# Attention blocks 2 to 4, tiles 20 to 29: two heads' sums of weights taken from pairs of tiles that GpSimd adds

## The chip, the cores and the metric

The kernel runs on one core of one Trainium2 chip. Times are device microseconds of that core. The chip runs five engines beside each other: TensorE (matrix products), VectorE, ScalarE, GpSimd and SyncE (which issues loads). They work on SBUF; TensorE writes its results to PSUM. The metric is the time of a whole execution, as the median over several runs.

## The reference, cut to what matters

A layer of graph attention with four heads over 4096 nodes, then a mixture of eight experts with the best two for each node. The change lies in the attention:

```python
h = jnp.einsum('nd,hdk->hnk', x, W)                     # 4 heads of 64
s_col = jnp.einsum('hnk,hk->hn', h, a1)
s_row = jnp.einsum('hnk,hk->hn', h, a2)
e = leaky_relu(s_row[:, :, None] + s_col[:, None, :], 0.2)
e = jnp.where(adj[None, :, :] > 0, e, NEG_INF)          # adj: 4096 x 4096 of 0 and 1
att = softmax(e, axis=-1)
h_prime = jnp.einsum('hij,hjk->hik', att, h)
```

So for each row i and head, two sums over the columns j are wanted: the weights times h (the numerator) and the weights alone (the denominator). Then follow an ELU, a residual, a layer norm, and for each node the choice of two experts, whose feed-forward results are added.

## The kernel before, in words

**Blocks and tiles.** The 4096 rows are worked in four blocks of 1024 (`NR = 4`; in the code block 1 is `a = 0`), each of two halves of 512. Over each block the kernel walks through 32 column tiles of 128 columns (`NT = 32`, index `j`). Columns lie on the partitions, rows along the free dimension.

**One tile.** SyncE loads 128 x 1024 of the transposed `adj` (`load_adj`, L1184). ScalarE turns it into a mask `am` in bfloat16, 0 or 2 (`mask_of`, L1606); there are three buffers. VectorE then makes the weights of one head at a time, for both halves together, in the order of heads 1, 0, 2, 3 (`weigh`, L1689): the larger of a row factor `er` and a column factor `eb`, cut by the mask. The exponentials have been split so that this needs no exponential in the loop; a factor that depends on the column alone is left out of the weights and is put on the other operand of the products, in `ha` (h of the column, times the factor) and `unit` (the factor alone, between columns of zeros). Weights `w` have ten buffers of 128 x 1024, that is two and a half tiles.

**The products.** For every tile, half and head TensorE multiplies `ha` by the weights (`rows_of_head`, L1198; two products of 32 columns each, added up in the four PSUM banks `acc`) and `unit` by the weights (`weights_of_head`, L1207; one product, added up in the bank `den`). [...] four products that use different columns can be under way together. An f32 product shows as two records, so a tile has 32 records of L1198 and 16 of L1207. `PLACE` says in which columns a head's sum of weights lies. The order of the products within a tile is written out by hand (`attend`) and chained by `queue`, so TensorE never changes it.

**What runs beside it.** While block n+1 is walked through, block n is finished a step at a time: `finish_blocks` is a generator, and after each tile the loop asks it for one more step (`next(pending)`). It divides (`shares_of`), applies ELU, residual and norms, and then routes (`route_rows`): transposes of the rows (L1253, evicted by L1256), the logits (L1264, evicted by L1269), their transposes (L1273), the choice of two experts on VectorE (L1280 to L1314), the place of each node in its expert's list (L1327 to L1345), and at last 16 indirect DMAs from GpSimd's queue that write the rows to the experts' lists in DRAM (L1385). In block 2, the first to be routed beside, a few steps more are made (two comparisons of 1024 elements, L1363). These steps take their PSUM from three shared banks with the tag `bank`.

**The order of work.** Apart from the chains written by hand, each engine's order is set when the program is built, by a planner that goes by the order in the code and its own estimates of time. On the chip each engine then works through its list in that order.

**Around it.** In block 4, after tile 3, a plan for the first experts is made and the rows of the first expert tile are loaded (L571); at tile 29 they are transposed (L607). After the attention comes the feed-forward phase, in which the last block is finished as well and its rows written to `xe`.

Of the kernel before, what the change touches and what calls it, by code (L numbers as in the profile page):

```python
# [18 lines left out]
P = 128  # L19
# [13 lines left out]
FINAL = (16, 15, 15, 15, 13, 13, 12, 9)  # L33
LIST = 36 * CH
PLACE = (2, 3, 0, 1)
ORDER = (1, 0, 2, 3)


# [6 lines left out]
def gat_then_moe(  # L45
# [173 lines left out]
    def forward(apart, stack):  # L219
# [16 lines left out]
        def first_large(name):  # L236
            return fin.tile([P, TB, D], F32, tag="first", name=name, bufs=2)
# [7 lines left out]
        def bank(shape, name):  # L245
            return ps.tile(shape, F32, tag="bank", name=name, bufs=3)
# [368 lines left out]
        with ExitStack() as layer:  # L615
# [588 lines left out]
            def weights_of_head(w, j, half, h):  # L1204
# [4 lines left out]
                    start=(j == 0 and half == 0), stop=(j == NT - 1 and half == HB - 1),  # L1209
                ))  # L1210

            def attend(w, j, halves, sums_first=None):


                def first_heads():
                    for half in halves:
                        for h in (1, 0):
                            rows_of_head(w, j, half, h)

                def other_heads():  # L1220
                    for half in halves:
                        for h in (1, 0):
                            weights_of_head(w, j, half, h)
                        rows_of_head(w, j, half, 2)
                    for half in halves:
                        rows_of_head(w, j, half, 3)
                        for h in (3, 2):
                            weights_of_head(w, j, half, h)

                parts = (first_heads, other_heads)  # L1230
                if sums_first is None:
                    sums_first = j in (0, NT - 1)
                for add in reversed(parts) if sums_first else parts:
                    add()

            def shares_of(pd):

                z = small.tile([P, TB, H, HB], F32, tag="z", name="z")
                for h in range(0, H, 2):
                    nc.vector.reciprocal(z[:, :, h : h + 2], pd[:, :, PLACE[h] : PLACE[h] + 2, :HB])  # L1240
                return z

            def route_rows(b, xe):
# [102 lines left out]
                if b == 0:  # L1346
# [33 lines left out]
                    yield  # L1380
                    nc.vector.tensor_tensor(others, others, least, OP.max)

                for t in range(n):
                    for k in range(2):
                        ins = nc.gpsimd.indirect_dma_start(  # L1385
                            lists, bass.IndirectOffsetOnAxis(ap=at[:, k, t : t + 1], axis=0),
                            xe[:, t, :], None,
                        ).ins
                        for i in listed:
                            tc.declare_no_dep(ins, i.name, reason="other places of the lists")  # L1390
                        listed.append(ins)

            def finish_blocks(a):
# [12 lines left out]
                for t in range(TB):  # L1406
                    order_of(nc.tensor.transpose(
                        pd[:, t].rearrange("p h q -> p (h q)"), ud[:, ts(t, P)], ident
                    ))
                z = shares_of(pd)  # L1410
                xe = rows_listed()
                n = HB * TB
                halves = [(half, slice(half * TB, (half + 1) * TB)) for half in range(HB)]
# [108 lines left out]
            def turn_sums(ud):  # L1522
                pd = bank([P, TB, H, Q], "pd")
                for t in range(TB):
                    queue(nc.tensor.transpose(
                        pd[:, t].rearrange("p h q -> p (h q)"), ud[:, ts(t, P)], ident
                    ))
                z = shares_of(pd)
                return z

            def last_block(b, u, z, given, xe):

# [146 lines left out]
            else:  # L1679

                with tc.tile_pool(name="sep", bufs=2) as work:

                    def weigh(er, am, j, halves):
# [10 lines left out]
                                w[half][h] = wh[:, half]  # L1694
                        return w

                    both = list(range(HB))
                    ers = [er0, er1]
                    er = er0
# [27 lines left out]
                        if j == 0:  # L1727
                            sums_turned(row)
                    for a in range(NR):
                        later = None  # L1730
                        for j in range(0 if a else TB, NT):
                            attend(
                                weigh(er, load_mask(a, j), j, both), j, both,
                                False if (a, j) == (NR - 1, NT - 1) else None,
                            )
                            if a == 0:
                                prepare_at(TB + j)
                            if pending:
                                next(pending, None)
                            if a == 1 and j == 1:  # L1740
                                turn_biases()
                            if a + 1 == NR and j == 3:
                                with tc.issue_after(marks["w"]):
                                    plan_early()
                                first_tile()
                            if a + 1 == NR and j == 29:
                                turn_first()
                                gelu_next(xT0[:, DC - 1, :1])
                            if j == 20 and a + 1 < NR:
                                later = ers[(a + 1) % 2]  # L1750
                                load_rows(later, (a + 1) * HB, HB, nc.scalar)
                        if a == 0:
                            mean_of_h()
                        er = later
                        if a + 1 < NR:
                            pending = finish_blocks(a)
                            next(pending)
# [351 lines left out]
```

## Time and profile before

| What | Value |
|---|---|
| Median of 3 runs | 1262.46 us (1262.27 to 1264.15) |
| The profiled execution's own time | 1260.56 us |
| Its span, first to last instruction | 1258.8 us |
| Granted TensorE clock | 0.999 |
| PE busy | 1241.7 us, 99% |
| DVE busy | 845.5 us, 67% |
| ACT busy | 448.3 us, 36% |
| POOL busy | 240.4 us, 19% |
| Attention, blocks 2 to 4, by TensorE's records | 256 to 782 us |

PE is TensorE, DVE VectorE, ACT ScalarE, POOL GpSimd, SP SyncE. In a line of the profile, L1198 is a line of the kernel, `out<-in` are tiles by the program's names, then come shapes and `xcount`. In a group's line the busy time, the mean of one in ns, and the engine's idle time before them with what ended it follow. In a line of the order of time the first number is the start in us, the second the length of the row, which may stand for several instructions one behind the other, and a bracket at the end holds the idle time before it and what ended that. Matmuls are pipelined and their ends are modelled, so that a busy PE isn't a PE at its peak.

### The profile page before, as it was taken

The page shows a single profiled execution, that of the slowest core. Times are in us where ns is not written, and L with a number is a line of the kernel's source. Part 1 is how long each engine was busy: PE and PEld are TensorE (multiplying, and loading weights), DVE is VectorE, ACT ScalarE, POOL GpSimd, SP SyncE. Part 2 cuts the span into 40 slices and gives each one's busy share as a digit, 9 for nine tenths or more (in the row PEclk, how much of TensorE's full clock was granted, in tenths as well). Part 3 has the DMA queues.
Part 4 walks back from the last instruction along what each step waited for, and adds up shares of the span by engine and source line. Part 5 has one row for each costly group of instructions (what it writes and reads, how often), then busy time and mean ns, then how long its engine had stood idle before and what let it go on. Part 6 is the DMA issues. An engine that isn't in the chain of part 4 may idle for free.

```text
span 1258.8 us, 22720 instructions
## 1 busy us (share of the span) xinstructions
PE 1241.7 (99%) x8872; PEld 650.4 (52%) x8872; DVE 845.5 (67%) x1566; ACT 448.3 (36%) x918; POOL 240.4 (19%) x217
## 2 busy tenths in 40 slices
PE   9999999999999999999999999999999999999997
PEld 5444444332233332333325324888888876666686
DVE  7998887879999999999999995855111111111120
ACT  4332322265522365322655221533332332222322
POOL 4000000001002601006110024125322222122222
PEclk9999999999999999999999999999999999999999
DMA  6334433536533646334375422868998895455662
GB/s 215 118 118 126 155 107 102 166 104 145 177 114 103 225 112 201 116 94 158 107 178 183 133 70 77 276 171 219 259 236 239 227 219 116 102 139 105 140 160 37
DMA packets 155541, 190.23 MB, mean 151 GB/s; under 512 B 72312, under 2 KB 125680, under 8 KB 155040
## 3 DMA queue, kind: packets, MB, share of 16 engines
q1 hardware_dynamic: 133392, 145.39, 39.7%
q0 software_dynamic: 20544, 36.74, 13.2%
q10 hardware_dynamic: 1488, 6.55, 1.4%
q8 instruction: 71, 1.16, 0.4%
q14 instruction: 46, 0.38, 0.1%
HBM read 155.77 MB, written 29.74 MB: 147 GB/s over the span
## 4 chain that ended last, share of the span: by engine, by line
PE 93%; DVE 3%; issue 1%; ACT 1%; DMA 1%; POOLq 0%; SPq 0%; DVEq 0%; ACTq 0%
PE acc L1198 33%; PE po L1906 18%; PE ph L1872 17%; PE den L1207 17%; PE pr L1053 2%; DVE w L1689 2%; PE ph L1101 2%; PE ptx L1253 0%; DMA early<-lists 0%; PE acc L894 0%; PE pt L780 0%; PE ptr L1491 0%; PE po L1945 0%; PE pl L1264 0%; PE po L875 0%
## 5 line engine op out<-in xcount | busy, mean ns | idle before, releaser
L1198 PE MATMUL acc<-w,ha 128*32 128x512 f32 x4096 | 672.1, 593 | 2.3 <-ACT u L1401 0.9
L1689 DVE SCALAR_TENSOR_TENSOR w<-er,eb,am 128x1024 f32<-128x1024 f32 x496 | 605.9, 1275 | 36.2 <-PE den L1207 30.3
L1207 PE MATMUL den<-w,unit 128*2 128x512 f32 x2048 | 469.2, 592 | 0.4 <-issue 0.3
L1198 PEld LDWEIGHTS acc<-w,ha 128*32 128x32 f32 x4096 | 186.7, 110 | 293.7 <-issue 254.3
L1606 ACT ACTIVATE am<-adj 128x1024 bf16<-128x1024 int32 x124 | 130.6, 1054 | 347.8 <-DVE w L1689 213.1
L1872 PE MATMUL ph<-xT,w 128*128 128x256 f32 (+5 forms) x864 | 230.2, 424 | 2.1 <-issue 1.9
L1906 PE MATMUL po<-w,hT 128*128 128x256 f32 (+1 forms) x1040 | 229.7, 379 | 0.0
L1876 ACT ACTIVATE hT<-ph,bias 128x256 f32<-128x256 f32 (+5 forms) x216 | 111.1, 517 | 290.2 <-issue 185.8
L1906 PEld LDWEIGHTS po<-w,hT 128*128 128x128 f32 (+1 forms) x1040 | 195.7, 189 | 31.2 <-issue 3.1
L1919 DVE SCALAR_TENSOR_TENSOR o<-po,share,b2s 128x256 f32<-128x256 f32 (+2 forms) x66 | 31.7, 482 | 250.2 <-PE po L1906 211.4
L1872 PEld LDWEIGHTS ph<-xT,w 128*128 128x128 f32 x864 | 163.4, 190 | 62.0 <-issue 40.3
L1207 PEld LDWEIGHTS den<-w,unit 128*2 128x2 f32 x2048 | 94.7, 85 | 148.5 <-issue 140.0
L1931 POOL DMA_INDIRECT out<-o,ids x66 | 102.0, 1546 | 321.9 <-DMA out<-o,ids 136.4
L1385 POOL DMA_INDIRECT lists<-xe,at x64 | 88.3, 1379 | 267.6 <-issue 184.7
L1856 DVE STREAM_TRANSPOSE xT<-xr 128x512 f32<-128x512 f32 (+5 forms) x21 | 17.8, 850 | 34.0 <-PE ph L1872 31.2
L1053 PE MATMUL pr<-wr,xT 128*128 128x256 f32 x128 | 30.4, 381 | 0.2 <-ACT er L1147 0.2
L1894 ACT ACTIVATE b2s<-b2b,share 128x256 f32<-128x256 f32 x68 | 30.1, 499 | 0.0
L1121 POOL DMA_DIRECT2D residual<-rb x6 | 4.7, 784 | 121.2 <-DVE rb L1068 121.2
L1441 POOL DMA_DIRECT2D xf<-in_x x6 | 8.1, 1351 | 102.2 <-ACT xf L1440 102.2
L1053 PEld LDWEIGHTS pr<-wr,xT 128*128 128x128 f32 x128 | 24.1, 190 | 5.4 <-issue 0.9
L1101 PE MATMUL ph<-wall,xT 128*128 128x264 f32 x96 | 24.6, 399 | 0.0
L207 ACT ACTIVATE m<-y,off 128x256 f32<-128x256 f32 x48 | 23.7, 495 | 1.1 <-DVE off L215 0.6
(394 smaller groups left out, 618.8 us busy)
## 6 DMA issues: line engine op xcount, KB each, us to landing
adj<-in_adj SPq DMA_DIRECT2D x126, 512.0 KB
w<-in_L_ffn_W SPq DMA_DIRECT2D x54, 1024.0 KB
er<-parts ACTq DMA_DIRECT2D x3, 2048.0 KB
lists<-zeros POOLq DMA_DIRECT2D x8, 520.0 KB
residual<-rb POOLq DMA_DIRECT2D x8, 512.0 KB
rb<-residual SPq DMA_DIRECT2D x8, 512.0 KB
out<-y POOLq DMA_DIRECT2D x8, 512.0 KB
xb<-in_x SPq DMA_DIRECT2D x7, 512.0 KB
```

Source lines behind the costliest of these rows:

```text
L1053: order_of(nc.tensor.matmul(pr[:, k, :], turned[b][:, c, ts(t0 + k, P)], wr[:, c, :], start=(c == 0), stop=(c == DC - 1),))
L1101: order_of(nc.tensor.matmul(phs[t - t0], xT[:, c, ts(t, P)], wall[:, c, :], start=(c == 0), stop=(c == DC - 1),))
L1198: queue(nc.tensor.matmul(acc[half][h // 2][here : here + Q, :], ha[:, j, h * K + g * Q : h * K + (g + 1) * Q], w[half][h], start=(j == 0), ...
L1207: queue(nc.tensor.matmul(den[here : here + HB, :], unit[:, j, h, 1 - half : 1 - half + HB], w[half][h], start=(j == 0 and half == 0), stop ...
L1385: ins = nc.gpsimd.indirect_dma_start(lists, bass.IndirectOffsetOnAxis(ap=at[:, k, t : t + 1], axis=0), xe[:, t, :], None,).ins
L1606: nc.scalar.activation(am, at, AF.Relu, scale=2.0)
L1689: marks["w"] = nc.vector.scalar_tensor_tensor(wh[:, these], er[:, these, h], eb[:, j, h : h + 1], mask[:, these], op0=OP.max, op1=OP.min,).ins
L1872: order_of(nc.tensor.matmul(ph, job["w1"][:, c, ts(f, P)], xT[:, c, :], start=(c == 0), stop=(c == DC - 1),))
L1876: job["gelu"] = nc.scalar.activation(hT[:, f, :], ph, AF.Gelu, bias=job["bias"][:, f : f + 1]).ins
L1906: order_of(nc.tensor.matmul(po[:size], hT[:, f, k * CH : k * CH + size], w2[:, f, :], start=(f == 0), stop=(f == FC - 1),))
L1919: given_out.append(nc.vector.scalar_tensor_tensor(o[:size], po[:size], share[:size, k : k + 1], b2s[k][:size], op0=OP.mult, op1=OP.add,).ins)
L1931: added.append(add().ins)
```

## The change

In blocks 2 to 4 every tile goes through new functions (`weigh_both`, `attend_both`), in block 1 none does. Three things are different.

First, the places of the sums of weights: each half has columns of its own now (`place_of`), and two heads share them. With that the order of the products in a tile is another: numerators of heads 1 and 0, then their sums of weights, then numerators of heads 2 and 3, then their sums. `shares_of` reads the new places.

Second, tiles 20 to 29 are taken as five pairs. In a pair the sums of weights of heads 1 and 0 are not made for each tile. Instead ScalarE multiplies the even tile's weights by the ratio of the two tiles' column factors (`ratio`), GpSimd adds the odd tile's weights (`added_pair`), and TensorE multiplies the odd tile's `unit` by that, once for each half and head, at the end of the odd tile. The added weights use two buffers of the tag `first`. In these tiles the mask is copied by ScalarE into one of two tiles of PSUM (`packed_mask`, two bfloat16 taken as one int32), which are two of the three shared banks, and VectorE reads it from there.

Third, the generator gives the word `"lists"` ahead of the list scatters, and the loop asks for the next step only from tile 30 on.

```diff
+PAIRED = (20, 30)
+ADDED = (1, 0)
...
+            def place_of(h, half):
+                return 2 * (h % 2) + half
+
+            def weights_by_half(w, j, half, h, start=False, stop=False):
+
+                here = place_of(h, half) * Q
+                queue(nc.tensor.matmul(
+                    den[here : here + HB, :], unit[:, j, h, 1 - h // 2 : 1 - h // 2 + HB],
+                    w[half][h], start=start, stop=stop,
+                ))
+
+            def attend_both(w, j, alone, summed=None, sums_first=False):
+
+                halves = range(HB)
+
+                def first_heads():
+                    for half in halves:
+                        for h in (1, 0):
+                            rows_of_head(w, j, half, h)
+
+                def other_heads():
+                    if alone:
+                        for h in (1, 0):
+                            for half in halves:
+                                weights_by_half(w, j, half, h, start=(j == 0))
+                    for half in halves:
+                        for h in (2, 3):
+                            rows_of_head(w, j, half, h)
+                    for h in (2, 3):
+                        for half in halves:
+                            weights_by_half(
+                                w, j, half, h, start=(j == 0 and not alone), stop=(j == NT - 1)
+                            )
+                    if summed:
+                        for h in ADDED:
+                            for half in halves:
+                                weights_by_half(summed, j, half, h)
...
+                if not ordered[0]:
+                    yield "lists"
                 for t in range(n):
                     for k in range(2):
                         ins = nc.gpsimd.indirect_dma_start(
...
+                    def packed_mask(am, j):
+
+                        pm = masks[j % 2]
+                        nc.scalar.copy(pm.bitcast(I32), am.bitcast(I32))
+                        return pm.bitcast(BF16)
+
+                    def weigh_both(er, a, j):
+
+                        am = load_mask(a, j)
+                        mask = packed_mask(am, j) if paired(j) else am
+                        w = [[None] * H for half in range(HB)]
+                        for h in ORDER:
+                            wh = work.tile([P, HB, B], F32, tag="w", name="w", bufs=10)
...
+                            made[j % 2][h] = wh
...
+                    def added_pair(j):
+
+                        w = [[None] * H for half in range(HB)]
+                        for h in ADDED:
+                            s = first_large("s").rearrange("p t d -> p (t d)")
+                            s = s.rearrange("p (s r) -> p s r", s=HB)
+                            nc.scalar.activation(
+                                s, made[0][h], AF.Copy, scale=ratio[:, j // 2, h : h + 1]
+                            )
+                            nc.gpsimd.tensor_tensor(s, s, made[1][h], OP.add)
+                            for half in range(HB):
+                                w[half][h] = s[:, half]
+                        return w
...
+                        if a == 1:
+                            pairs = unit[:, :, :2, 1].rearrange("p (n k) h -> p n k h", k=2)
+                            nc.vector.tensor_scalar(ratio, pairs[:, :, 1], TINY, None, op0=OP.max)
+                            nc.vector.reciprocal(ratio, ratio)
+                            nc.vector.tensor_tensor(ratio, ratio, pairs[:, :, 0], OP.mult)
+                            nc.vector.tensor_scalar(ratio, ratio, 1.0 / EPS, None, op0=OP.min)
...
+                            if a == 0:
+                                attend(weigh(er, load_mask(a, j), j, both), j, both)
+                            else:
+                                if j == PAIRED[0]:
+                                    masks = [bank([P, B], "pm") for k in range(2)]
+                                w = weigh_both(er, a, j)
+                                attend_both(
+                                    w, j, not paired(j),
+                                    added_pair(j) if paired(j) and j % 2 else None,
+                                    j == 0 or j == NT - 1 and a + 1 < NR,
+                                )
...
-                            if pending:
-                                next(pending, None)
+                            if pending and (step != "lists" or j >= PAIRED[1]):
+                                step = next(pending, None)
```

More of the change, by code (lines that the diff above doesn't have):

```diff
@@ L1210, in weights_of_head @@
                 ))
+            def place_of(h, half):
[29 more added lines that the diff above has]
+                                weights_by_half(summed, j, half, h)
+                parts = (first_heads, other_heads)
+                for add in reversed(parts) if sums_first else parts:
+                    add()
             def attend(w, j, halves, sums_first=None):
@@ L1234, in attend, with shares_of @@
                     add()
-            def shares_of(pd):
+            def shares_of(pd, by_half):
                 z = small.tile([P, TB, H, HB], F32, tag="z", name="z")
+                if by_half:
+                    for k in range(0, H, 2):
+                        nc.vector.reciprocal(
+                            z[:, :, k : k + 2].rearrange("p t h s -> p t (h s)"), pd[:, :, :, k // 2]
+                        )
+                    return z
                 for h in range(0, H, 2):
@@ L1409, in finish_blocks @@
                     ))
-                z = shares_of(pd)
+                z = shares_of(pd, apart and a > 0)
                 xe = rows_listed()
@@ L1527, in turn_sums @@
                     ))
-                z = shares_of(pd)
-                return z
+                return shares_of(pd, apart)
             def last_block(b, u, z, given, xe):
@@ L1695, in weigh, with paired @@
                         return w
+                    def paired(j):
+                        return PAIRED[0] <= j < PAIRED[1]
+                    def packed_mask(am, j):
[8 more added lines that the diff above has]
+                            wh = work.tile([P, HB, B], F32, tag="w", name="w", bufs=10)
+                            marks["w"] = nc.vector.scalar_tensor_tensor(
+                                wh, er[:, :, h], eb[:, j, h : h + 1],
+                                mask.rearrange("p (s r) -> p s r", s=HB), op0=OP.max, op1=OP.min,
+                            ).ins
+                            made[j % 2][h] = wh
+                            for half in range(HB):
+                                w[half][h] = wh[:, half]
+                        return w
[8 more added lines that the diff above has]
+                            nc.gpsimd.tensor_tensor(s, s, made[1][h], OP.add)
+                            for half in range(HB):
+                                w[half][h] = s[:, half]
+                        return w
+                    made = [[None] * H for k in range(2)]
+                    ratio = gat.tile([P, NT // 2, 2], F32)
                     both = list(range(HB))
@@ L1729, in forward @@
                     for a in range(NR):
[L1730 to L1735 removed]
+                        later, step = None, None
+                        if a == 1:
[4 more added lines that the diff above has]
+                            nc.vector.tensor_scalar(ratio, ratio, 1.0 / EPS, None, op0=OP.min)
+                        for j in range(0 if a else TB, NT):
+                            if a == 0:
[8 more added lines that the diff above has]
+                                    j == 0 or j == NT - 1 and a + 1 < NR,
+                                )
                             if a == 0:
                                 prepare_at(TB + j)
[L1738 to L1739 removed]
+                            if pending and (step != "lists" or j >= PAIRED[1]):
+                                step = next(pending, None)
                             if a == 1 and j == 1:
```

## The prediction

> **What bounds the kernel now.** I read the groups first, then the order of time on TensorE, VectorE, ScalarE and GpSimd through blocks 2 to 4 (256 to 782 us), last the chain. The groups name the two engines that matter: the products of the attention, and the weighting on VectorE that feeds them.
>
> ```profile
> L1198 PE MATMUL acc<-w,ha 128*32 128x512 f32 x4096 | 672.1, 593 | 2.3 <-ACT u L1401 0.9
> L1689 DVE SCALAR_TENSOR_TENSOR w<-er,eb,am 128x1024 f32<-128x1024 f32 x496 | 605.9, 1275 | 36.2 <-PE den L1207 30.3
> L1207 PE MATMUL den<-w,unit 128*2 128x512 f32 x2048 | 469.2, 592 | 0.4 <-issue 0.3
> ```
>
> A mean of 593 ns for a product is no price: four of them run side by side. The price is the distance from tile to tile, in TensorE's order of time where nothing else lies between:
>
> ```profile
> 571.92 1.90 PE L1198 MATMUL acc<-w,ha 128*32 128x512 f32 x16
> ...
> 577.07 1.90 PE L1198 MATMUL acc<-w,ha 128*32 128x512 f32 x16
> ...
> 582.22 1.90 PE L1198 MATMUL acc<-w,ha 128*32 128x512 f32 x16
> ```
>
> A tile takes 5.15 us for 48 records (each f32 product is two), four at a time: 12 slots of 0.429 us. VectorE's order of time gives its price per weighting and what else it does:
>
> ```profile
> 509.29 33.56 DVE L1689 SCALAR_TENSOR_TENSOR w<-er,eb,am 128x1024 f32<-128x1024 f32 x28
> 543.70 3.68 DVE L1689 SCALAR_TENSOR_TENSOR w<-er,eb,am 128x1024 f32<-128x1024 f32 x3 [0.84 <-PE den L1207]
> ...
> 554.77 0.21 DVE L1291 TENSOR_TENSOR oh<-lg,mm 128x64 f32<-128x64 f32 x1
> 554.90 0.15 DVE L1306 TENSOR_TENSOR d<-mm 128x8 f32<-128x8 f32 x1
> 555.02 0.23 DVE L1294 TENSOR_TENSOR oh<-oh,order 128x64 f32<-128x64 f32 x1
> ```
>
> 28 weightings in 33.56 us are 1.20 us each (the 1275 ns overlap), so 4.79 us a tile, plus small routing operations. So the engines are nearly level: TensorE sets the time, VectorE is only 0.36 us a tile faster, and loses that where routing or finishing falls to it. What keeps TensorE fed is a **head start**. I measure it as TensorE's first product of a tile minus the end of the tile's fourth weighting, counting four weightings and 48 records to a tile. In block 3 it is 3.85 us at tile 0, -2.08 at tile 9 (finishing work on VectorE), 4.37 at tile 20, 4.18 at tile 30. Block 2 has 4.58 at tile 20 and 3.12 at tile 30. Block 4 has 3.81 at tile 0, then -3.16 at tile 5 and -4.00 at tile 9, and there TensorE does wait for VectorE:
>
> ```profile
> 655.22 0.62 PE L1198 MATMUL acc<-w,ha 128*32 128x512 f32 x2 [0.40 <-DVE w L1689]
> ```
>
> VectorE's only slack is its waits for a free weight buffer (ten of them), as the 0.84 us above: at the head of block 3 they are 0.25, 1.67 and 1.44 us, at the head of block 4 0.25 and 1.68.
>
> [...] four products per 0.429 us slot. [...] The trace has no GpSimd arithmetic here, but its scatters fit: their issues last 2.08 us or 0.97, and the difference of 1.1 is about one weighting (two SBUF inputs).
>
> ```profile
> 578.35 2.08 POOL L1385 DMA_INDIRECT lists<-xe,at  x1 [0.30 <-issue]
> 580.73 0.97 POOL L1385 DMA_INDIRECT lists<-xe,at  x1 [0.30 <-issue]
> ```
>
> [...] start to start, the three-operand operation on 256 elements takes 395 ns from PSUM (L1063) and 397 from SBUF (L1564). [...]
>
> **The change part by part.** *Removed.* In a pair the sums of heads 1 and 0 go from 8 products to 4: 2 slots, 0.857 us. 15 pairs give 12.9 us, 4.29 a block. All of it is on the path while the head start lasts.
>
> *Order of products, tiles of blocks 2 to 4.* Still 12 slots, four columns filled in each: nothing. But heads 2 and 3 are now both wanted from slot 7, 2.57 us after the tile's start (head 3, made last, was wanted from slot 9, 3.43 us), and in paired tiles from slot 5, 1.71 us. So TensorE waits once the head start falls below about -2.6, or -1.7 in a pair.
>
> *Weighting with its mask in PSUM.* 120 of them; by the trace 0 more each. [...]
>
> *GpSimd's adds*, [...] the last is due at slot 11 of the odd tile. With head 1 of that tile weighted 1.7 us before the tile starts, [...] and the sum is wanted 4.29 us in. Hidden; it shows above about 3 us an add. Queued behind them on GpSimd are only the scatters.
>
> *Collisions.* The weightings no longer have two SBUF inputs, but routing has: the rows at 554.77 to 555.02 are such, and they fall into tiles 22 to 24, where the adds run. [...] I count two adds met in blocks 3 and 4 each (2.2 us) and four in block 2, whose tile 27 also has the two 1024-element comparisons L1363 (4.4 us). Ends: 0 to twice that.
>
> *ScalarE.* Per tile one copy of the mask into PSUM (0.58 us, the row of 512 elements at L1256), per pair two scalings of 1.06 us as L1606: 3.3 us more per pair of some 10 us, on an engine that is busy 10 to 13 us of the 55 in that stretch. The scalings wait for `s`, so for the pair before to end; masks queue behind them, and VectorE behind those. At a head start of 8 us for the first weighting this costs at most about 1.5 us a block, and it costs nothing once the start has shrunk; 0 to 1.5.
>
> *Scatters to tile 30.* The 16 issues take 25 to 33 us on GpSimd (572 to 601 in block 3) and begin some 13 us later, behind the adds; they end by tile 3 of the next block. Who wants them: the load of the first expert's rows on SyncE's queue at 632 us, and in the last block the rewriting of `xe` at 812, each more than 15 us after the new end; GpSimd's next own work comes at 627. Nothing. Reciprocals, ratios (four tiny operations once): nothing.
>
> **The sum**, as a ledger of the head start. *Block 2's pairs:* 3.12 - 4.29 - 4.4 = -5.6; floor -1.7, so TensorE waits 3.9. *Head of block 3:* from -1.7, +0.73 to tile 0 as before, is 4.8 below the old; the buffer waits vanish and give 3.4 back; tile 9 is at -2.08 - 1.4 = -3.5; floor -2.6: waits 0.9. *Block 3's pairs:* 4.37 - 0.5, -0.2 to tile 30 as before, +1.1 of vanished buffer waits, -4.29 - 2.2, is -1.7: no wait. *Head of block 4:* 4.9 below the old, 1.9 given back; tiles 5 to 9 have no room: waits 3.0. *Block 4's pairs:* 4.2 + 0.4 - 4.29 - 2.2 = -1.9: 0.2. Waits together 8.0; what is left of 12.9 is 4.9 us. Not every collision will be met; [...] and I take 5.5. The profiled execution took 1260.56 us (span 1258.8 and 1.8 around it), so 1255.1; the median of the runs is 1.9 above it, and the same gain gives **1257.0**.
>
> **The rivals.**
> *All of it stays:* collisions and ScalarE cost nothing, the adds are hidden. Then only the head of block 4 gives back, 1 to 3 us: 10 to 12, about 1251. For it: buffer waits of 3.4 and 1.9 us. Against: the routing rows lie where the adds run.
>
> *No change:* [...] about 1263. Against: 395 beside 397 ns.
>
> *Slower: masks wait for a bank.* Three banks are shared; two are now masks for ten tiles. VectorE starts tile 20 at 530.82, long before TensorE. But the transposes and logits of tiles 18 and 19 hold banks till later, until these rows end:
>
> ```profile
> 536.73 1.05 ACT L1256 COPY xT<-ptx 128x512 f32<-128x512 f32 x2
> ...
> 541.51 0.41 ACT L1269 COPY lT<-pl 128x128 f32<-128x128 f32 x2
> ```
>
> If banks are given in the order of the program, tile 20's mask waits until about 537.8 and tile 21's until 541.9: VectorE is 7 us late and the head start is gone before the first pair. In the ledger each block then waits 6 us more at its pairs (7 less the buffer wait of about 1 that vanishes): 18 in all against 5.5 gained, 12 slower, about 1275; half the delay, 3.5 us, gives about 1264. It decides from about 3 us. Against: the banks are free before tile 17, and masks prepared ahead could take them then; the routing would queue for the one left.
>
> *The sum isn't shortened* (other slots run empty): then nothing is gained and the waits stay; counted with the slower case.
>
> **How the numbers follow.** 0.2%, or 2.5 us, is about what a measurement of this kernel can tell from no change. Forecast (gain of 2.5 to 8) 0.44; all stays (over 8) 0.18; no change 0.14; slower 0.24, among it adds of over 3 us. So faster 0.62, same 0.14, slower 0.24. The range goes from 1250.5 (12 us gained, the whole removal less 0.9) to 1267.0, which leaves out the worse part of the banks' case.
>
> **What would show it.** Den records: 60 products, 120 records, fewer. Weightings in tiles 20 to 29 still 1.20 us apart. [...] The routing rows in tiles 22 to 24 with gaps or lengths of 1 to 2 us. Even paired tiles 4.29 us apart. Head start near -1.7 at tile 30 and TensorE waiting for w at tiles 5 to 9 of block 4. Wrong if the head start falls before tile 20, if adds take over 3 us, or if weightings from PSUM stand further apart.

## The result: 5.5% slower

The changed kernel takes 1331.56 us, the kernel before 1262.37 us beside it: a ratio of 1.0552 (95% interval 1.0531 to 1.0574). The prediction was 1257.0 us, range 1250.5 to 1267.0. The profiled execution took 1331.96 us (span 1330.2). Where the 71.4 us between the two spans lie, from the first product of tiles 0, 20, 27 and 30 in TensorE's order of time, summed over blocks 2 to 4, in us:

| | tiles 0-19 | 20-26 | 27-29 | 30-31 | attention ends at | span behind it |
|---|---|---|---|---|---|---|
| before | 330.8 | 111.6 | 49.0 | 34.4 | 781.9 | 476.9 |
| after | 334.4 | 130.3 | 96.1 | 33.0 | 849.6 | 480.6 |

Two thirds come in three tiles a block, 27 to 29, a quarter in tiles 20 to 26. The groups of the profile after (line engine op out<-in xcount | busy us, mean ns | idle before us and its releasers):

```profile
L1764 DVE SCALAR_TENSOR_TENSOR w<-er,eb,am 128x1024 f32<-128x1024 f32 x264 | 329.5, 1311 | 29.7 <-POOL s L1782 21.8 <-PE den L1220 7.2 <-PE den L1209 0.6
L1764 DVE SCALAR_TENSOR_TENSOR w<-er,eb,pm 128x1024 f32<-128x1024 f32 x120 | 147.1, 1274 | 15.8 <-ACT pm L1754 15.8
L1782 POOL TENSOR_TENSOR s<-s,w 128x1024 f32<-128x1024 f32 x30 | 70.6, 2372 | 217.3 <-DVE w L1764 180.7 <-DVE first L1346 21.5 <-DVE oh L1341 14.9
L1220 PE MATMUL den<-s,unit 128*2 128x512 f32 x120 | 31.2, 678 | 36.8 <-POOL s L1782 36.8
```

Products (L1200) and single sums wait little more than before; the new products, the sums of `s`, do: 36.8 us for GpSimd's adds (L1782). An add takes 2372 ns, so its length isn't the reason. Its place is. GpSimd's order of time in block 3:

```profile
603.06 1.04 POOL L1437 DMA_INDIRECT lists<-xe,at  x1 [4.41 <-DVE at L1395]
...
609.54 0.97 POOL L1437 DMA_INDIRECT lists<-xe,at  x1 [0.30 <-issue]
610.54 4.68 POOL L1782 TENSOR_TENSOR s<-s,w 128x1024 f32<-128x1024 f32 x2
615.39 1.00 POOL L1437 DMA_INDIRECT lists<-xe,at  x1 [0.16 <-issue]
...
619.24 7.04 POOL L1437 DMA_INDIRECT lists<-xe,at  x1 [0.31 <-issue]
...
632.97 0.97 POOL L1437 DMA_INDIRECT lists<-xe,at  x1 [0.30 <-issue]
633.95 4.65 POOL L1782 TENSOR_TENSOR s<-s,w 128x1024 f32<-128x1024 f32 x2
```

In block 3 six scatters stand in front of the adds of tiles 26 and 27, ten in front of those of tiles 28 and 29, and one of the ten lasts 7.04 us. The hold to tile 30 sits in the order of the program; the order in which GpSimd gets its work is the planner's. The first scatter goes out as soon as its indices `at` are there, and the adds come behind. (That the planner expected the adds later is likely, but not shown.) TensorE, in order, stops at the sum (11.48 us in its order of time, at the end of tile 29):

```profile
636.36 1.87 PE L1220 MATMUL den<-s,unit 128*2 128x512 f32 x4 [11.48 <-POOL s L1782]
```

and with it VectorE, whose weight buffers are not given back (its own order of time):

```profile
636.34 4.55 DVE L1764 SCALAR_TENSOR_TENSOR w<-er,eb,am 128x1024 f32<-128x1024 f32 x2 [10.91 <-POOL s L1782]
```

TensorE's waits for `s`, 36.8 us, all lie in tiles 27 to 29. A part of the rest of the loss there is the clock: from 421.9, 630.1 and 828.1 us, within the waits, the granted clock is 0.50 for 10.24 us each. In the kernel before it is 1.00 all through the attention. In the second of these stretches groups of products start 0.81 us apart, as the first two at 636.36 and 637.17 do, and a record lasts 1.01 to 1.06 us; at 1.00 it is 0.43 and 0.59. TensorE is busy for 12.9 us of the three stretches; by these distances about half of that, 6.5 us, is an estimate of what the lower clock costs.

Tiles 20 to 26 are lost on VectorE, in its order of time in block 3:

```profile
535.40 19.22 DVE L1764 SCALAR_TENSOR_TENSOR w<-er,eb,am 128x1024 f32<-128x1024 f32 x16
558.76 4.86 DVE L1764 SCALAR_TENSOR_TENSOR w<-er,eb,pm 128x1024 f32<-128x1024 f32 x4 [4.14 <-ACT pm L1754]
568.30 0.23 DVE L1330 TENSOR_TENSOR lg<-pg,bgb 128x64 f32<-128x64 f32 x1 [4.67 <-PE pg L1323]
569.07 9.62 DVE L1764 SCALAR_TENSOR_TENSOR w<-er,eb,pm 128x1024 f32<-128x1024 f32 x8 [0.55 <-ACT pm L1754]
...
581.25 1.39 DVE L1344 TENSOR_TENSOR oh<-oh,order 128x64 f32<-128x64 f32 x1
...
592.67 1.78 DVE L1361 TENSOR_SCALAR p<-th 128x8 f32<-128x8 f32 x1 [0.62 <-ACT th L1359]
```

Tile 20 waits 4.14 us for its mask. In ScalarE's order of time the copy of the mask follows directly on the last eviction of a transpose, and the next ones come behind those of the logits:

```profile
557.04 1.07 ACT L1306 COPY xT<-ptx 128x512 f32<-128x512 f32 x2 [0.31 <-PE ptx L1303]
558.14 0.59 ACT L1754 COPY pm<-am 128x512 int32<-128x512 int32 x1
...
563.68 0.27 ACT L1319 COPY lT<-pl 128x128 f32<-128x128 f32 x1 [0.17 <-PE pl L1314]
...
566.88 0.58 ACT L1754 COPY pm<-am 128x512 int32<-128x512 int32 x1
...
568.45 0.58 ACT L1754 COPY pm<-am 128x512 int32<-128x512 int32 x1
```

In the code the masks ask for their banks behind the transposes, so the bank is the likely reason; the trace can't tell it from the copy's place in ScalarE's own queue. Then a routing operation, `lg`, stands ahead of tile 21's weightings and waits 4.67 us for a product on TensorE. The weightings wait 0.55 us more, for a copy that ends at 569.03, so in this kernel the mask ends last here too. Together 9.4 us: the head start of block 3, 4.37 us at tile 20 before, is -0.2, and -3.5 at tile 21. Once a mask is there, eight weightings take 9.62 us, 1.20 each, as much as in the kernel before (28 in 33.56 us): here a mask in PSUM costs no more than one in SBUF. The last two rows of VectorE are operations that meet an add; in the kernel before they take 0.23 and 0.17 us.

### The profile page after: what moved, and what is told of

The parts are those of the page before. It is cut to its first block, busy times and chain, and to the rows that moved or that the text cites. A ratio compares the mean times of both kernels' runs of the same rounds, so it can differ in the third digit from the quotient of the medians.

```text
span 1330.2 us, 22649 instructions
## 1 busy us (share of the span) xinstructions
PE 1262.9 (95%) x8752; PEld 667.0 (50%) x8752; DVE 860.4 (65%) x1570; ACT 498.0 (37%) x978; POOL 300.0 (23%) x247
## 4 chain that ended last, share of the span: by engine, by line
PE 83%; POOL 5%; DVE 4%; issue 4%; ACT 2%; DMA 1%; POOLq 0%; SPq 0%; DVEq 0%; ACTq 0%
PE acc L1200 28%; PE po L2011 17%; PE ph L1977 16%; PE den L1220 9%; PE den L1209 4%; DVE w L1764 3%; POOL lists L1437 3%; PE pr L1055 2%; PE ph L1103 2%; POOL s L1782 2%; ACT s L1779 1%; PE ptx L1303 1%; DMA early<-lists 0%; PE acc L896 0%; PE pt L782 0%
## 5 line engine op out<-in xcount | busy, mean ns | idle before, releaser
L1200 PE MATMUL acc<-w,ha 128*32 128x512 f32 x4096 | 579.2, 600 | 8.8 <-DVE w L1764 7.2
L1764 DVE SCALAR_TENSOR_TENSOR w<-er,eb,am 128x1024 f32<-128x1024 f32 x264 | 329.5, 1311 | 29.7 <-POOL s L1782 21.8
L1200 PEld LDWEIGHTS acc<-w,ha 128*32 128x32 f32 x4096 | 169.9, 110 | 299.5 <-issue 214.7
L1220 PE MATMUL den<-w,unit 128*2 128x512 f32 x1296 | 201.1, 592 | 0.0
L1764 DVE SCALAR_TENSOR_TENSOR w<-er,eb,pm 128x1024 f32<-128x1024 f32 x120 | 147.1, 1274 | 15.8 <-ACT pm L1754 15.8
L1740 DVE SCALAR_TENSOR_TENSOR w<-er,eb,am 128x1024 f32<-128x1024 f32 x112 | 138.3, 1276 | 13.3 <-PE den L1209 13.3
L1782 POOL TENSOR_TENSOR s<-s,w 128x1024 f32<-128x1024 f32 x30 | 70.6, 2372 | 217.3 <-DVE w L1764 180.7
L1209 PE MATMUL den<-w,unit 128*2 128x512 f32 x512 | 117.6, 592 | 0.1
L1220 PEld LDWEIGHTS den<-w,unit 128*2 128x2 f32 x1296 | 45.4, 85 | 94.1 <-issue 79.6
L1437 POOL DMA_INDIRECT lists<-xe,at x64 | 76.4, 1193 | 31.5 <-issue 17.4
L1220 PE MATMUL den<-s,unit 128*2 128x512 f32 x120 | 31.2, 678 | 36.8 <-POOL s L1782 36.8
L1779 ACT ACTIVATE s<-w,ratio 128x1024 f32<-128x1024 f32 x30 | 33.1, 1144 | 42.1 <-PE den L1220 42.1
L1209 PEld LDWEIGHTS den<-w,unit 128*2 128x2 f32 x512 | 23.5, 85 | 38.8 <-issue 37.7
```

Of the source, the lines that this page charges most:

```text
L1200: queue(nc.tensor.matmul(acc[half][h // 2][here : here + Q, :], ha[:, j, h * K + g * Q : h * K + (g + 1) * Q], w[half][h], start=(j == 0), ...
L1209: queue(nc.tensor.matmul(den[here : here + HB, :], unit[:, j, h, 1 - half : 1 - half + HB], w[half][h], start=(j == 0 and half == 0), stop ...
L1220: queue(nc.tensor.matmul(den[here : here + HB, :], unit[:, j, h, 1 - h // 2 : 1 - h // 2 + HB], w[half][h], start=start, stop=stop,))
L1437: ins = nc.gpsimd.indirect_dma_start(lists, bass.IndirectOffsetOnAxis(ap=at[:, k, t : t + 1], axis=0), xe[:, t, :], None,).ins
L1740: marks["w"] = nc.vector.scalar_tensor_tensor(wh[:, these], er[:, these, h], eb[:, j, h : h + 1], mask[:, these], op0=OP.max, op1=OP.min,).ins
L1764: marks["w"] = nc.vector.scalar_tensor_tensor(wh, er[:, :, h], eb[:, j, h : h + 1], mask.rearrange("p (s r) -> p s r", s=HB), op0=OP.max, ...
```

## The experiments

In the expectations, theory A is that scatters ahead of the adds cost the time, theory C that the masks wait for a bank; the third candidate is that adds and VectorE keep each other out at SBUF. Sums in us over blocks 2 to 4 as above; ratios to the kernel before that ran beside each (medians of 1254 to 1263 us):

| | ratio (95%) | 20-26 | 27-29 | behind |
|---|---|---|---|---|
| e1, scatters behind adds | 1.0292 (1.0254-1.0331) | 130.6 | 48.4 | 488.8 |
| e2, order only | 1.0034 (1.0010-1.0059) | 111.6 | 47.5 | 478.4 |
| e3, masks only | 1.0372 (1.0329-1.0416) | 120.6 | 82.3 | 477.0 |
| e4, e1 from tile 22 | 1.0136 (1.0103-1.0168) | 116.2 | 48.4 | 486.7 |
| e5, e1 with masks in SBUF | 1.0515 (1.0479-1.0552) | 140.7 | 68.8 | 482.9 |
| e6, no hold | 1.0564 (1.0547-1.0581) | 130.3 | 94.9 | 478.1 |
| e7, e3 with fills | 1.0186 (1.0153-1.0220) | 120.7 | 48.7 | 486.7 |
| e8, e4 with fills | 1.0237 (1.0205-1.0268) | 116.2 | 48.4 | 501.4 |
| e9, before with fills | 1.0028 (1.0016-1.0040) | 111.6 | 47.5 | 481.9 |
| e10, blocks 2, 3 from tile 24 | 1.0105 (1.0087-1.0123) | 119.9 | 46.6 | 475.1 |
| e11, tiles 10 to 15 | 1.0050 (1.0034-1.0066) | 111.6 | 47.5 | 476.6 |
| e12, tiles 8 to 17 | 1.0084 (1.0059-1.0108) | 113.8 | 47.5 | 476.7 |
| e13, before, five fills | 0.9966 (0.9955-0.9977) | 111.6 | 47.4 | 478.1 |
| e14, masks only, 10 to 15 | 1.0020 (1.0008-1.0032) | 111.6 | 47.5 | 479.7 |

**e1: the scatters behind the last add.**

```diff
-                            nc.gpsimd.tensor_tensor(s, s, made[1][h], OP.add)
+                            marks["add"] = nc.gpsimd.tensor_tensor(s, s, made[1][h], OP.add).ins
...
-                        ins = nc.gpsimd.indirect_dma_start(
+                        with tc.issue_after(marks["add"]) if "add" in marks and not ordered[0] else ExitStack():
+                            ins = nc.gpsimd.indirect_dma_start(
```

> The changed kernel with one ordering edge more: in each block the 16 list scatters stand behind the last add of tile 29 on GpSimd's queue. Theory A (GpSimd's queue: scatters planned ahead of the adds of tiles 27 and 29 hold TensorE there, some 49 us over three blocks): 1280 to 1292 us, TensorE's waits for s below 3 us a block, the scatters start only after the tenth add. Rival B (the chain of scaling, add and sum is too long by itself, whatever stands in the queue): above 1310 us, tiles 27 and 29 still over 8 us long.

Tiles 27 to 29 go from 96.1 us to 48.4; TensorE's wait for `s` is gone, and the lower clock in these tiles with it: theory A is shown, at 48 us. About 8 of them come back behind the attention (488.8 us for 480.6), where the scatters of block 4 now run, and so the time, 1293.55 us, is just above the forecast.

**e2: the new order alone** (`paired` is always false, no mask banks, the hold kept).

> The changed kernel with no pairs, no adds and no masks in PSUM; the new places and the new order of the products stay, and the hold of the scatters. Theory A and theory C (the masks in PSUM start VectorE's tile 20 late for want of a bank): both say the order costs nothing, 1259 to 1265 us. Rival D (heads 2 and 3 being wanted earlier in a tile costs TensorE waits in blocks 2 to 4): 1266 us or more, with tiles over 5.4 us at tiles 5 to 17.

At most 0.6%: places, order and reciprocals are not the cause. The hold is in this kernel too, and still its scatters of block 3 begin at 573.24 us, against 572.02 before. So the hold doesn't delay them.

**e3: masks in PSUM for tiles 20 to 29, no pairs, no adds.**

```diff
-                        return PAIRED[0] <= j < PAIRED[1]
+                        return False
...
-                        mask = packed_mask(am, j) if paired(j) else am
+                        mask = packed_mask(am, j) if PAIRED[0] <= j < PAIRED[1] else am
```

> The changed kernel with the masks of tiles 20 to 29 copied to PSUM, but no pair and no add: every tile has its own sums. Theory C: the weighting of tile 20 or 21 still begins late, VectorE idles 8 to 10 us a block there, and with nothing saved on TensorE the time is 1272 to 1284 us. Rival: it is the scaling on ScalarE that delays the masks, so without it the masks come in time: 1260 to 1266 us and no idle time of VectorE at tile 20.

Tiles 20 to 26 lose 9.0 us in three blocks, and in block 3 VectorE idles 10.9 us there, with no scaling in the program: the delay of theory C, at a lower cost than expected. It has two parts. Tile 20 waits 5.41 us for its mask; then `lg` waits 5.53 us for TensorE, until 560.63, while the next two masks are done by 558.44, so here `lg` ends last. The time as a whole is above both forecasts. The surprise is 33 us in tiles 27 to 29, with no add in the program. There the scatters follow one another at 1.28 us, where in the kernel before about half of them stand some 2.4 us apart, and TensorE has holes that no semaphore explains (releaser "issue"), all while scatters are issued. TensorE's order of time in block 3:

```profile
605.26 0.63 PE L1200 MATMUL acc<-w,ha 128*32 128x512 f32 x2 [1.08 <-issue]
607.36 1.31 PE L1200 MATMUL acc<-w,ha 128*32 128x512 f32 x3 [1.47 <-issue]
609.50 1.03 PE L1200 MATMUL acc<-w,ha 128*32 128x512 f32 x2 [0.82 <-issue]
```

e2 has such holes too, smaller: in block 3 its last ten scatters come 1.27 to 1.46 us apart, and tiles 30 and 31 take 15.1 us instead of 10.3. e7, e9 and e13 are about these.

**e4: e1 with** `PAIRED = (22, 30)`, where the transposes have let go of their banks.

> As e1_behind_adds, and the pairs begin at tile 22 (four instead of five), after the transposes and logits of the routing have given their banks back. Theory C: the head start is kept at tile 22 and VectorE does not idle there more than 3 us a block; TensorE saves 10.3 us less the waits of the ledger: 1256 to 1265 us. Rival: the head start is lost to the routing's collisions and to ScalarE anyway: 1268 us or more.

14.4 us less in tiles 20 to 26 than e1, with one pair fewer. But the forecast of theory C fails, in the time (1275 us) and in what it said of VectorE: the head start is not kept. In blocks 3 and 4 it is 0.1 us at tile 22. The masks of tiles 22 and 23 are there in time for `lg`, and `lg`, ahead of tile 22's weightings, waits for TensorE (ScalarE's and VectorE's order of time, block 4):

```profile
724.36 1.12 ACT L1755 COPY pm<-am 128x512 int32<-128x512 int32 x2
...
728.28 0.22 DVE L1330 TENSOR_TENSOR lg<-pg,bgb 128x64 f32<-128x64 f32 x1 [5.26 <-PE pg L1323]
```

So the masks are one part of the delay, and the order on VectorE's own queue is another. The kernel is still slower than before, and most of that now lies behind the attention: the first 32 products of the feed-forward layer take 18.9 us (787.34 to 806.27; 7.17 before), with "issue" holes, beside scatters that run to 798 us. The granted clock, 0.50 from 792.4 to 806.1 us, has a share in it.

**e5: e1 with the masks read from SBUF** (`mask = am`, no mask banks).

> The kernel with the scatters behind the last add, but the weightings of tiles 20 to 29 read their masks from SBUF as before, so no bank is waited for. If a weighting with two SBUF inputs and a GpSimd add keep each other out, a pair costs VectorE 8 x 1.20 us + 2 x 2.37 us = 14.3 us where TensorE needs 9.4 us: five pairs take 72 us, less some 6 us of head start, so tiles 20 to 29 last 64 to 70 us a block (59 to 61 us with masks in PSUM) and the time is 1305 to 1325 us. If the two do not meet, only the wait for the bank is gone: 52 to 54 us for tiles 20 to 29, time 1265 to 1275 us.

As the first case said: 209.5 us for tiles 20 to 29 where e1 needs 179.0, though no bank is waited for. Both sides pay. GpSimd's order of time in block 3 has four adds in 20.6 us:

```profile
553.25 20.61 POOL L1783 TENSOR_TENSOR s<-s,w 128x1024 f32<-128x1024 f32 x4 [46.96 <-DVE w L1765]
```

and VectorE's, in the same stretch, a weighting of over 3 us:

```profile
562.71 3.27 DVE L1765 SCALAR_TENSOR_TENSOR w<-er,eb,am 128x1024 f32<-128x1024 f32 x1
```

**e6: the change without its hold** (the two lines `if not ordered[0]: yield "lists"` taken out).

> The changed kernel without the hold of the list scatters alone. By the theory that the place in the program does not keep the scatters behind the adds, the planned order on GpSimd is what counts: here 6 adds, all 16 scatters, then 4 adds in blocks 3 and 4, so one long wait for s at tile 27 (or 29) in place of two: 1320 to 1340 us, like the changed kernel's 1331 us. If the hold is what delays the adds, 1280 to 1300 us.

The same time as with it: GpSimd then has all 16 scatters in one piece (601.4 to 621.6 us in block 3) ahead of the last four adds. The hold neither caused nor prevented the wait, as e2 says too.

**e7: e3 with a fill on GpSimd behind each scatter.**

```diff
+                        if not ordered[0]:
+                            with tc.issue_after(ins):
+                                last = nc.gpsimd.memset(idle, 0.0).ins
```

> Masks in PSUM without pairs and adds, and behind each list scatter a GpSimd fill of 128x1024 (about 1 us) that does nothing else, so that scatters stand about 2.3 us apart and not 1.27 us. If scatters 1.27 us apart are what stalls the engines in tiles 27 to 29, the stage 27 to 30 goes back from 26 to 29 us to 15 to 18 us in each block and the time falls from 1303 us to 1265 to 1277 us. If it is something else of the masks in PSUM (their copies, the banks, the order on VectorE), the time stays at 1298 to 1306 us.

Only a 0.97 us fill and the edges that chain it to the scatters are added on GpSimd, and tiles 27 to 29 fall from 82.3 to 48.7 us. So the holes depend on how closely the scatters follow. The spacing isn't the fill's alone: in each block one scatter lasts long, 24.6, 23.4 and 10.2 us, and those behind it come later. The time itself is above what was expected: 10 us more are lost behind the attention, where the scatters now end at 805 us.

**e8: e4 with the fills.**

> Pairs from tile 22, scatters behind the adds, and the same 1 us fill behind each scatter. If scatters 1.27 us apart stall the first products of the feed-forward layer (16.8 to 18.8 us for 32 products that take 7.2 us in the kernel before), that goes, and 8 to 10 us of the 1275 us with it: 1263 to 1269 us; scatters that end near 811 us may then hold up the first write of the output, up to 5 us. If the loss there has another cause: 1273 to 1280 us.

A miss, and an instructive one. The 32 first products are back at 7.43 us, but then TensorE waits for a load (the view of waits: us in total, times, longest us):

```profile
PE pt L609 <- DMA b2b<-in_L_ffn_b: 18.2, 1, 18.2
```

and that load stands on SyncE's queue behind another that waits (the waits of that queue, 770 to 830 us):

```profile
SPq L573 <- DMA lists<-xe,at: 20.2, 3, 16.2
```

The load `early<-lists` (L573) wants the scatters of block 4, which end at 811 us; everything behind it on SyncE waits too. In the kernel before that load is issued at 783.87 us, when the scatters have been out since 770.

**e9: the kernel before with the fill** behind the last ten scatters of each block.

> The kernel before, with the 1 us fill behind the last ten of the 16 list scatters of each block. In block 4 of the kernel before VectorE has nothing to weigh from 764 us on, the scatters come 1.27 us apart, and tiles 27 to 31 last 31.4 us where block 3 needs 25.8 us. If the spacing is the cause, 3 to 6 us of that come back: 1251 to 1254 us against 1257 us. If not: 1256 to 1258 us, or a little more for scatters that end later.

Tiles 27 to 31 of block 4 take 26.7 us instead of 31.4, as expected, so the kernel before had such holes as well. The forecast of the time fails all the same: 5 us more are lost behind the attention, where `early<-lists` goes out at 790.77. That the attention ends at 782.1 us as before says nothing against the fills. The profiled execution was 4.8 us slower than the median of its runs: the granted clock was 0.50 from 8.8 and from 261.4 us, 10.2 us in all, and at tile 20 of block 2, ahead of all fills, it was 4.9 us behind the kernel before.

**e10: e1 with** `PAIRED = (24, 30)`, in blocks 2 and 3 only; block 4 with masks in SBUF, its scatters free.

> Pairs in blocks 2 and 3 only and from tile 24 only (three pairs each), scatters there behind the last add; block 4 with masks from SBUF, sums one by one and no chain on the scatters. If banks, the scatters ahead of adds and the late lists of block 4 are all that costs, six pairs save 6 x 0.86 = 5.1 us, of which collisions with the routing and the smaller head start take 1 to 4: 1252 to 1257 us against 1256 us. If the adds and the scalings cost more by themselves[...]: 1259 to 1266 us.

The first case fails: the time, 1266 us, is at the upper end of the second. Nothing is lost behind the attention any more, but tiles 20 to 26 still lose 8.3 us: VectorE now waits 7.63 us at the routing's `rank`, ahead of tile 25's weightings, for a product on TensorE. The next masks are copied by 566.03, so the wait has moved to the next routing operation (VectorE's order of time, block 3):

```profile
572.42 0.23 DVE L1385 TENSOR_TENSOR rank<-pk,filled 128x64 f32<-128x64 f32 x1 [7.63 <-PE pk L1377]
```

**e11 and e12: the change with** `PAIRED = (10, 16)` and `(8, 18)`, nothing else.

> The changed kernel with its pairs in tiles 10 to 15 instead of 20 to 29 and nothing else altered: no bank is wanted by the routing or the finishing there, the list scatters come ten tiles later, VectorE runs few routing operations. If the pairs were spoilt by what they met (banks, scatters, late lists), they now do what they say: 9 pairs remove 7.7 us from TensorE, of which VectorE, nearly level, lets 4 to 7 through: 1248 to 1253 us against 1255 us. If masks in PSUM, scalings and adds are dear in themselves: 1258 us or more.

> The same with pairs in tiles 8 to 17, as many as the change has (15). The finishing of the block before reaches tile 9 and the transposes of the routing start at tile 17, so both ends touch the places where banks are wanted. If banks decide, this gives no more than the pairs in tiles 10 to 15, and 1 to 6 us less when a mask waits: 1250 to 1258 us. If only the number of pairs counted: 1244 to 1249 us.

e11 ends in its second case, and e12 in neither of its own: no bank is disputed in e11, and still tiles 0 to 19 take 3.4 us more than before, not less. The pair does what it says on TensorE, whose order of time shows an even tile of 4.29 us (485.35 to 489.64):

```profile
485.35 3.62 PE L1200 MATMUL acc<-w,ha 128*32 128x512 f32 x32
488.78 1.04 PE L1220 MATMUL den<-w,unit 128*2 128x512 f32 x8
489.64 2.76 PE L1200 MATMUL acc<-w,ha 128*32 128x512 f32 x24
```

But VectorE needs 32.4 us from tile 10's first weighting to tile 16's in block 2, where the kernel before needs 29.5: 3.0 us lost for 2.57 removed (3.0 and 3.3 in blocks 3 and 4). They are a 1 us wait for a mask, whose copy stands on ScalarE behind work that waited for a load, and two operations on eight elements that meet adds (VectorE's order of time):

```profile
334.73 1.41 DVE L163 TENSOR_TENSOR q<-r 128x8 f32<-128x8 f32 x1
...
337.25 1.22 DVE L164 SCALAR_TENSOR_TENSOR q<-q,v 128x8 f32<-128x8 f32 x1
```

In e12, tiles 0 to 19 take 11.9 us more in three blocks than before: masks waited for, weightings with masks in SBUF that meet the last adds (2.77, 2.74 and 2.47 us in place of 1.27), and in block 2 a granted clock of 0.50 for 3.4 us, which the pairs don't explain.

**e14: e3 with** `PAIRED = (10, 16)`, the masks of e11 without its adds.

> Masks in PSUM for tiles 10 to 15 only, no pairs, no scalings, no adds; everything else as changed. If the pairs of tiles 10 to 15 lost their 2.6 us a block to VectorE operations that met the adds, those tiles' weightings now stand as close as in the kernel before (29.5 us from the first of tile 10 to the first of tile 16 in block 2, where with pairs they took 32.4 us), and the time is within 3 us of the order alone, 1.003 of the kernel before. If it was the masks in PSUM or their copies on ScalarE, the 32 us stay and the time is 1.006 or more.

30.0 us for the same stretch, with the 0.9 us wait for a mask; the two small operations last 0.16 us again. So in block 2 2.4 of e11's 3.0 us come with the scalings and adds. In blocks 3 and 4 the masks alone need 30.4 and 30.9 us, with waits of 1.3 and 1.8 us for a mask, and 2.1 and 1.6 us are left for scalings and adds.

**e13: the kernel before with five fills,** in block 4 only, behind the seventh to the eleventh scatter.

```diff
+                        if b == (NR - 2) * HB and not ordered[0] and 6 <= 2 * t + k < 11:
+                            with tc.issue_after(ins):
+                                last = nc.gpsimd.memset(idle, 0.0).ins
```

> The kernel before, with the 1 us fill only in block 4 and only behind five scatters (the seventh to the eleventh), so that their end moves from 770 to about 775 us, still ahead of the attention's end. If scatters 1.27 us apart stall the engines there and late lists cost the rest of what the earlier fills lost, 2 to 5 us come back: ratio 0.996 to 0.998. If the fills themselves cost something: 1.000 or more.

0.9966 (0.9955 to 0.9977): faster than both kernels. It is within the forecast. The attention ends at 776.8 us, 5.1 earlier, and the scatters at 775.5, still ahead of it. In the groups, VectorE's idle time ahead of weightings falls from 36.2 us to 30.5:

```profile
L1695 DVE SCALAR_TENSOR_TENSOR w<-er,eb,am 128x1024 f32<-128x1024 f32 x496 | 605.9, 1276 | 30.5 <-PE den L1207 30.5
```

## Why the prediction was wrong, point by point

- *Scatters to tile 30 … behind the adds … Nothing.* The step that failed, and the largest: it put the cost at nothing, and e1 gives 48 us back, 36.8 of them TensorE's waits for `s`. It took the place in the program for the place in the queue, although the section on the order of work says that a planner sets it. "Queued behind them on GpSimd are only the scatters" named the right neighbours in the wrong order. "Begin some 13 us later" failed with it: in e2 the hold moves the scatters by 1.2 us. Its list of who wants the scatters missed `early<-lists`, at 783.87 us in the kernel before; that did not strike the change itself, but e8, where it cost 18 us.
- *Slower: masks wait for a bank.* The rival that came true, with 7 us late at the first pair against 9.4 measured, and 18 us in all; tiles 20 to 26 lost 18.7. That the two sums come so close is luck: masks alone cost 9.0 us there (e3), and the rest came with the pairs, on a VectorE that now set the pace. Its argument against, that masks could take the banks before tile 17, was wrong, and the range left its worse part out for it. What it lacked is VectorE's own order, `lg` ahead of the weightings: in e3 and e4 that wait ends last.
- *Collisions.* Right in kind, too small in scope. What a meeting costs, in the 2.2 and 4.4 us as in the 5.5 taken at the end, was the author's estimate; no row of before shows one. In each block two routing operations lose 1.2 and 1.6 us, 2.8 for the 2.2 forecast in blocks 3 and 4 and the 4.4 in block 2. Left out were weightings with masks in SBUF that meet late adds at tiles 30 and 31 (4.7 and 3.4 us for 1.27), and above all the conclusion: the sum let VectorE lose half of what TensorE gains, and e11 shows it loses all (3.0 us for 2.57), masks and adds together, with routing and scatters out of the way. On this head start the pairs had nothing to win.
- *The sum.* From -1.7 at tile 30 of block 3, against 4.18 before, the head of block 4 is 5.9 us below the old, not 4.9. With that the waits are 9.0 us and the gain 1 us less, which is small beside the steps above.
- *Weighting with mask in PSUM,* 0 more each: right, 1274 ns and 1.20 us start to start, 1275 before. That PSUM takes longer, as the rival *no change* had it, is not seen in these runs.
- *GpSimd's adds:* 2372 ns, below the 3 us from which they were to show. Their length in the prediction was the author's estimate, with no row of before behind it. By the measured mean two of them, begun 1.7 us before the odd tile, end 3.0 us into it, and the sum is wanted at 4.29: "Hidden" holds for their length. *Removed:* 120 records of sums fewer, even tiles 4.29 us apart in e11: right. Four at a time is what the trace of before shows: at 571.92 four records of L1198 start within 0.02 us, the next four 0.43 us later, and each lasts 592 ns.
- *SBUF inputs and adds.* A weighting with one SBUF input inside an add takes 1268 to 1277 ns (16 of them in the changed kernel; 1275 in the kernel before). With two both sides pay: single weightings of 3.23 to 3.42 us for 1.28, and adds of 3928 ns in the mean (e5). `p` (L1361) has one SBUF input and still lost 1.6 us in each block: it takes 1.78 us in block 3 in place of 0.17 and ends at 594.45, where the add ends at 594.43; so in the other blocks. The prediction counted only operations with two, which no row of before shows to be the ones that meet adds; why `p` waits and a weighting with one doesn't is not shown.
- *ScalarE*, 0 to 1.5 us a block: 1.0 us in e11 and 0.9 to 1.8 in e14, right in size.
- Not foreseen at all: the engines' holes while scatters come closely.

What stays open is how close scatters stop other engines. The trace shows 16 KB packets on a DMA queue that the profile calls instruction. In blocks 2 to 4 of the kernel before they stand 8.6 to 18.9 us apart; in e3, while TensorE has its holes, one comes at 616.3 us, 25.1 after the one before. Whether the late packet is a cause of the holes or follows from them is not shown. And close scatters don't always stop engines: e10's block 4 had ten of them 1.27 us apart, from 773.13 us on, and TensorE has no hole there, and in the changed kernel TensorE's waits in tiles 27 to 29 are for `s` alone. That the spacing matters is shown (82.3 us in tiles 27 to 29 of e3, 48.7 in e7; 5.1 us in block 4 of e13); how it acts is open.

## What to carry to other kernels

Where a planner orders each engine's queue, a position in the program held nothing back (scatters of block 3 from 573.24 us in e2, 572.02 before; e6); an edge to the instruction that must come first did (e1, 48 us). Before trusting a "hidden" step one reads who stands ahead of it in its own queue. An engine that is nearly level with the bound must not pay for the bound's relief: here masks and adds took from VectorE what the pairs saved TensorE (3.0 us for 2.57 in block 2 of e11). And a series of GpSimd scatters was a cost of its own here: how closely it comes (33.6 us in tiles 27 to 29 between e3 and e7) and when it ends (18.2 us of wait for a load in e8) both moved the time.

## What the runs showed of the hardware that was not expected

- An operation on 8 elements (128x8) with two SBUF inputs took 1.41 us in place of 0.15 beside a GpSimd add; a weighting with two SBUF inputs took 4.71 us across two adds (435.34 us in the changed kernel). The 1.41 us (e11) end at 336.14, about where the first of two adds ends (333.73 to 338.45 us for both), and the 1.22 us of the next small operation at 338.47, with the second: what was left of the add counted, not the operation's own length.
- Weightings at SBUF also go with slower scatters on GpSimd: 2.0 to 2.1 us each beside weightings with two SBUF inputs (the kernel before), 0.97 with masks in PSUM (e3). About half of the scatters of the kernel before were kept apart in this way (23 of 48 in blocks 2 to 4 last 1.9 to 2.1 us); e3 took it away.
- Single scatters last long: 23.4 us in e7 (598.34 in block 3) and 7.04 us in the changed kernel, between others of 0.97. What they waited for the profile doesn't say.
- With TensorE's long waits came a lower clock: in the changed kernel the granted clock fell to 0.50 within the wait, for 10.24 us in each block, and 3.4 to 6.0 us of work fell into that time.
